# Projecting a context in 64-row tiles: three chunks of 64 dims in place of 128 and 64, and copies shared by two engines

## The chip, the cores and the metric

The kernel runs on one core of one Trainium2 chip. The metric is the time of one execution in device microseconds (us). The engines named below are TensorE (PE in the profile, with its weight loads as PEld), VectorE (DVE), ScalarE (ACT), GpSimd (POOL) and SyncE (SP, which only issues transfers here).

## The reference, cut to what matters

The program is a model of four layers over x, 128 tokens of 256 numbers. Each layer has an attention over a long context, an attention among the tokens, and experts. All is fp32.

```python
x = x + _L0_xattn_ref(_layernorm(x), ctx_768, mask, Wq, Wk, Wv, Wo)
x = x + _L0_attn_ref(...) ; x = x + _L0_ffn_ref(...)
x = x + _L1_xattn_ref(_layernorm(x), ctx_768, Wq, bq, Wk, bk, Wv, bv, Wo, bo)
...                                   # layers 1, 2 and 3 likewise
```

The context `ctx_768` has 12544 rows of 192 numbers and is the same in all layers. An attention over it makes, for 16 heads of 16 numbers (layers 0 to 2), keys = ctx @ Wk (+ bk) and values = ctx @ Wv (+ bv), both 12544 x 256, then softmax(q k) v over all 12544 rows. Layer 0 has a mask, layer 1 clips its scores, layers 1 and 2 have biases. Layer 3 has heads of 64 numbers and its own code.

## The kernel before, in words

The context is cut into 25 blocks of 512 rows (`NSB`, `SB`), the last with 256. Heads go in two groups `g` of eight, whose keys are 128 rows of numbers. For each group `attend_twice_in` goes over the blocks twice. The first pass projects keys and values of each block, keeps them in SBUF, and finds the highest score of each query. The second pass makes the exponentials and the weighted sums from the kept keys and values.

*The projection* (class `Keys`, one matmul line, L103). A block's 192 dims lie in SBUF as two tiles: `ctxA` holds dims 0 to 127 on 128 partitions, and `ctxB` holds dims 128 to 191 of the block's first 256 rows on partitions 0 to 63 and of its second 256 rows on partitions 64 to 127. `keys_into` and `values_into` are called with `low` 0 (contract over 128 partitions) and then with `low` 1 (over 64, where the matmuls of the two halves use different partitions of the array). Keys of the first 256 rows go to the left half of one PSUM bank, their values to the right half, and the second 256 rows to a second bank: the tile `pair` of two banks. `keep_keys` (L131 without bias, L133 with) and `keep_values` (L137) then copy both banks to SBUF on ScalarE. Before the first pass, `early` projects two blocks (layer 0) or eight (layers 1 and 2) ahead, through the one-pair tile `kv`, in the midst of the work of the stage before; there the context comes by POOL's queue.

*The first pass.* `steps` says which blocks each step projects: two blocks ahead, and in group 0 of layers 1 and 2 fewer than one a step, since eight are done. The last three blocks project keys alone in their step and values later (`project_values`). Products with the queries (L559, L558 with the mask) are four matmuls of 32 rows side by side. In layer 0 each block's products go to VectorE, which takes maxima (L565, four a step). In layers 1 and 2 two blocks go together: POOL subtracts their keys (`apart`, L570), PE makes products with the difference, ScalarE takes a Relu of each of two pairs (`over`, L578), PE makes products with the second block's keys, and VectorE adds and takes the maximum (L586, four a step).

*What sets the order.* Tiles and their waits come from a tile framework; within a step, `in_order` holds PE, VectorE and ScalarE to the order in which the code names the work. The PSUM tiles of the first pass are a pool of four pairs (`ppr=4`), given out in turn: in layers 1 and 2 a step takes one for the projection, two for the difference, and two for the second keys. Outside the passes a scheduler places the instructions of each engine, from its own costs.

*Transfers.* `context` loads blocks one ahead into four buffers for each of `ctxA` and `ctxB` (L395 and L397). In layer 1, `add_up` adds each block of group 0 to `sums` on POOL (L99, L100), for a test on NaN in `nan_guard`. Layer 3 (`KeysInTurn`) takes its context from the same function, two blocks ahead. SP's queue also issues layer 0's mask rows (L547, four a block) and, at the start, layer 3's small weights (`down`, L1158), which VectorE scales between its first maxima. In layer 0's experts POOL makes eight widened copies (`wide`, L1691) that PE then turns, and the expert weights come by SP's queue into ten buffers.

Of the kernel before, what the change touches and what calls it, by code (L numbers as in the profile page):

```python
# [12 lines left out]
F32 = mybir.dt.float32  # L13
# [4 lines left out]
ALU = mybir.AluOpType  # L18
# [3 lines left out]
P = 128  # L22
D = 256
CD = 192
CB = CD - P
H = 16
# [27 lines left out]
class Keys:  # L54
# [4 lines left out]
    def __init__(self, net, wk, wv, groups, bias=None, sums=None):  # L59
        self.net, self.nc, self.wk, self.wv, self.bias, self.sums = net, net.nc, wk, wv, bias, sums  # L60
        self.context = net.context(groups * NSB)
        self.started, self.done, self.rest = {}, 0, None
        if sums is not None:
            self.nc.gpsimd.memset(sums, 0.0)
# [30 lines left out]
    def add_up(self, g, b):  # L95
        if g == 0 and self.sums is not None:
            a, c = self.context(b)
            n = HB * len(self.halves(b))
            self.nc.gpsimd.tensor_tensor(self.sums[:, :n], self.sums[:, :n], a[:, :n], ALU.add)  # L99
            self.nc.gpsimd.tensor_tensor(self.sums[:, SB:], self.sums[:, SB:], c, ALU.add)  # L100
# [16 lines left out]
    def values_into(self, p, g, low, blocks, first=0, turn=None):  # L117
        cols = slice(g * P, g * P + P)
        for j, b in enumerate(blocks):
            ctx = self.context((g if turn is None else turn) * NSB + b)[low]  # L120
            for c in range(2):
                for i, r in self.halves(b):
                    at = first + (2 * j + c) * P
                    r = r if low else slice(0, P)
                    k = c * P if low else i * HB + c * P
                    self.mm(p[:, i, at : at + P], ctx[r, k : k + P], self.wv[r, low, cols], low, first + j + c == 0)

    def keep_keys(self, g, b, p):
        to = self.kT(b).rearrange("p (i k) -> p i k", i=2)[:, : p.shape[1]]
        if self.bias is None:  # L130
            self.nc.scalar.copy(to, p)  # L131
        else:
            self.nc.scalar.activation(to, p, AF.Identity, bias=self.bias[:, g : g + 1])  # L133

    def keep_values(self, g, b, p):
        to = self.v(b).rearrange("p (i c) h e -> p i (c h) e", i=2)[:, : p.shape[1], :, :16]
        self.nc.scalar.copy(to, p.rearrange("p i (h e) -> p i h e", e=16))  # L137

    def steps(self, g):

        todo = [b for b in range(2, NSB) if g * NSB + b >= self.done]
        n, at, out = len(todo), 0, []
        for t in range(NSB):
            to = min(n, -(-n * (t + 1) // (NSB - 2)))
            while to < n and todo[to] <= t + 2:
                to += 1
            out.append([(b, low, b < NSB - 3) for b in todo[at:to] for low in range(2)])
            at = to  # L150
        return out

    def project(self, g, b, low, values=True):


        if g * NSB + b < self.done:
            return
        if not low:
            self.add_up(g, b)
            self.started[g, b] = self.net.early_pair() if self.rest is None else self.net.pair()  # L160
        p = self.started[g, b]
        self.keys_into(p, g, low, [b])
        if values:
            self.values_into(p, g, low, [b], HB)
        if low:
            n = len(self.halves(b))
            self.keep_keys(g, b, p[:, :n, :HB])
            if values:
                self.keep_values(g, b, p[:, :n, HB:])
            self.done = g * NSB + b + 1  # L170

    def project_values(self, g, blocks):
        p = self.net.pair()
        for low in range(2):
            self.values_into(p, g, low, blocks)
        for j, b in enumerate(blocks):
            self.keep_values(g, b, p[:, : len(self.halves(b)), j * HB : (j + 1) * HB])


class KeysInTurn(Keys):  # L180

    def __init__(self, net, wk, wv):
        self.net, self.nc, self.wk, self.wv = net, net.nc, wk, wv
        self.context = net.context((GROUPS3 + 1) * NSB, 2)
        self.first = {}
# [17 lines left out]
class Net:  # L207
# [123 lines left out]

    def load_column(self, src, pool, name):

        t = pool.tile([P, 2], F32, tag=name, name=name, bufs=1)
        self.nc.sync.dma_start(t, src.rearrange("o (g p) -> p (o g)", p=P))
        return t
# [46 lines left out]
    def context(self, until, ahead=1):  # L383

        nc, d = self.nc, self.d
        made = []

        def get(k):  # L390
            while len(made) <= k + ahead and len(made) < until:
                b = len(made) % NSB
                n = min(SB, S2 - b * SB)
                a = self.ahead.tile([P, SB], F32, tag="ctxA", name="ctxA", bufs=4)
                self.queue.dma_start(a[:, :n], d["ctxA"][:, b * SB : b * SB + n])  # L395
                c = self.ahead.tile([P, HB], F32, tag="ctxB", name="ctxB", bufs=4)
                self.queue.dma_start(c, d["ctxB"][b])  # L397
                made.append((a, c))
            return made[k]

        return get
# [617 lines left out]
    def l0_xattn(self, x):  # L1019
        nc, d = self.nc, self.d  # L1020
        with self.tc.tile_pool(name="x0", bufs=2, reuse_waits="tile") as pool:
            wk = self.load_kv(d["L0_xattn_Wk"], D, "wk", self.lw, nc.scalar)
            keys = Keys(self, wk, None, 2)
            keys.context(0)
            keys.wv = self.load_kv(d["L0_xattn_Wv"], D, "wv", self.lw, nc.scalar)
# [14 lines left out]
    def keys_biased(self, name, guarded):  # L1040

        nc, d = self.nc, self.d
        wk = self.load_kv(d[f"{name}_Wk"], D, "wk", self.lw)
        wv = self.load_kv(d[f"{name}_Wv"], D, "wv", self.lw)
        bk = self.load_column(d[f"{name}_bk"], self.lw, "bk")
        sums = self.lw.tile([P, SB + HB], F32, tag="sums", name="sums", bufs=1) if guarded else None
        keys = Keys(self, wk, wv, 2, bk, sums)

        self.queue = nc.gpsimd
        keys.early()  # L1050
        return keys
# [33 lines left out]
    def nan_guard(self, pool, totals, xT, wq, bq, wk, wv, bk, bv):  # L1085
# [4 lines left out]
        wide = pool.tile([P, 2, P], F32, tag="wide", name="wide")  # L1090
# [5 lines left out]
        def sums():  # L1096
            s = self.stat(2)
            nc.vector.tensor_reduce(s[:, 0:1], totals[:, :SB], AX.X, ALU.add)
            nc.vector.tensor_reduce(s[:, 1:2], totals[:, SB:], AX.X, ALU.add)
            nc.vector.tensor_copy(wide, bc(s, 2, P))  # L1100
            nc.gpsimd.memset(many, float(S2))

        def products(bank_pair):
            p = bank_pair()
            self.mm(p[:, 0, :D], [(xT[:, k, :], wq[:, k, :]) for k in range(2)] + [(self.ones[:1, :], bq)])
            self.mm(p[:, 1, :D], [(wide[:, k, :], wk[:, k, :]) for k in range(2)] + [(many, bk)])
            made.append(p)
            p = bank_pair()
            self.mm(p[:, 0, :D], [(wide[:, k, :], wv[:, k, :]) for k in range(2)])
# [749 lines left out]
def layout(inputs):  # L1859
# [4 lines left out]
    ctx[:, :S2] = a["ctx_768"][0].T  # L1864
    given["ctxA"] = ctx[:P, :S2]
# [31 lines left out]
def program(given):  # L1897
    nc = bacc.Bacc("TRN2", target_bir_lowering=False, num_devices=1)
# [12 lines left out]
```

## Time and profile before

| | us |
|---|---|
| median of 3 runs | 3020.04 (3013.86 to 3021.88) |
| profiled execution: time | 3021.48 |
| profiled execution: span | 3019.8 |
| PE busy (weight loads beside it) | 2882.8 (2209.0) |
| VectorE / ScalarE / POOL busy | 2024.2 / 1626.2 / 282.7 |
| start of a regular step to the next, first pass, layer 0 | 5.62 |
| the same, layers 1 and 2 | 5.42 |
| the same, keys-only steps of layers 1 and 2 | 3.99 |

The first passes of layer 0 run from about 40 to 160 and 275 to 420, of layer 1 from 658 to 785 and 906 to 1045, of layer 2 from 1311 to 1440 and 1554 to 1697. Experts of layer 0 end at about 650, layer 3 begins at about 1930.

How to read it: a row of the timeline gives the start, the length from the first start to the last end, engine, line, operation, the tiles (out<-in), for matmuls the rows and columns of the array in use (64\*128 is 64 rows), and a count. Idle time of the engine just before it and what ended that wait stand in brackets. An fp32 matmul is two instructions, and each has its own weight load (PEld). Matmuls are pipelined: the next starts before the last has ended, so starts tell the pace.

### The profile page before, as it was taken

The numbers are of one execution on the slowest core, as the hardware profiler recorded it, in microseconds if no ns is written. First come the engines' busy times: TensorE is split into PE (matmuls) and PEld (weight loads), VectorE is DVE, ScalarE is ACT, GpSimd is POOL, SyncE is SP. The second block draws the span as 40 slices with busy tenths as digits, with TensorE's granted clock in tenths as the row PEclk, the third lists the DMA queues.
The fourth block names the chain that finished last, engine by engine and source line by source line (L and its number), as shares of the span: only waits on it lengthen the run. The fifth ranks groups of instructions, "written<-read, shape, count | busy, mean of one in ns | idle before, by whom it ended". The sixth has DMA issues, their size and how long they took to land.

```text
span 3019.8 us, 79794 instructions
## 1 busy us (share of the span) xinstructions
PE 2882.8 (95%) x34893; PEld 2209.0 (73%) x34893; DVE 2024.2 (67%) x3241; ACT 1626.2 (54%) x1904; POOL 282.7 (9%) x504
## 2 busy tenths in 40 slices
PE   8999999989999999999999998899999999999969
PEld 5677667455676576765776675688989989889858
DVE  6876887525893598745544555577777777777844
ACT  1176148335685585245875682355655656555521
POOL 7011021223001100211001002000000000000000
PEclk9999999999999999999999998999999999999979
DMA  5201210562002202521012007232322223222436
GB/s 133 61 19 32 72 39 6 189 225 57 21 3 79 59 4 88 175 82 53 15 39 73 23 3 258 92 98 80 85 84 83 85 79 88 85 78 83 136 111 201
DMA packets 177706, 247.28 MB, mean 82 GB/s; under 512 B 32459, under 2 KB 119269, under 8 KB 177358
## 3 DMA queue, kind: packets, MB, share of 16 engines
q1 hardware_dynamic: 165592, 227.26, 24.8%
q0 software_dynamic: 11008, 14.37, 1.6%
q8 instruction: 274, 4.49, 0.6%
q10 hardware_dynamic: 758, 0.55, 0.1%
q14 instruction: 74, 0.61, 0.1%
HBM read 241.56 MB, written 0.13 MB: 80 GB/s over the span
## 4 chain that ended last, share of the span: by engine, by line
PE 83%; DVE 11%; ACT 2%; DMA 1%; issue 1%; SPq 1%; POOL 0%; ACTq 0%; DVEq 0%; POOLq 0%
PE pair L103 21%; PE acc L699 10%; PE pair L559 8%; PE v L103 8%; PE sc L859 6%; PE pair L629 5%; PE acc L901 5%; PE ps L279 5%; PE one L629 4%; DVE parts L565 3%; PE pair L622 2%; PE acc L279 2%; PE kv L103 2%; PE ps L1698 1%; DVE over L586 1%
## 5 line engine op out<-in xcount | busy, mean ns | idle before, releaser
L586 DVE CUSTOM_DVE_ANT_0 over<-over,pair 128x512 f32<-128x512 f32 x384 | 241.2, 683 | 249.2 <-PE pair L559 237.6
L103 PE MATMUL pair<-ctxA,wk 128*128 128x256 f32 x1236 | 328.7, 399 | 6.5 <-ACT over L578 1.8
L103 PEld LDWEIGHTS pair<-ctxA,wk 128*128 128x128 f32 x1236 | 217.0, 190 | 138.5 <-ACT over L578 53.0
L861 ACT COPY kept<-sc 128x1024 f32<-128x1024 f32 (+1 forms) x135 | 136.2, 1009 | 261.2 <-PE sc L859 261.2
L565 DVE TENSOR_REDUCE parts<-pair 128x2 f32<-128x1024 f32 (+1 forms) x216 | 235.7, 1157 | 41.8 <-PE pair L559 41.8
L290 DVE TENSOR_TENSOR top<-top,kept 128x1024 f32<-128x1024 f32 (+2 forms) x145 | 169.1, 1169 | 134.0 <-ACT kept L861 132.7
L293 DVE SCALAR_TENSOR_TENSOR e<-pair,floor 128x1024 f32<-128x1024 f32 x196 | 227.3, 1217 | 14.6 <-PE pair L629 14.6
L677 ACT ACTIVATE e<-pair 128x1024 f32<-128x1024 f32 x196 | 200.7, 1025 | 46.5 <-PE pair L629 26.0
L654 ACT ACTIVATE e<-e 128x1024 f32<-128x1024 f32 x196 | 206.7, 1057 | 35.3 <-DVE e L293 24.3
L629 PE MATMUL pair<-qz,kT 32*128 32x256 f32 x2112 | 218.9, 374 | 0.0
L699 PE MATMUL acc<-e,v 128*17 128x128 f32 x6336 | 211.4, 274 | 3.0 <-ACT e L692 2.2
L699 PEld LDWEIGHTS acc<-e,v 128*17 128x17 f32 x6336 | 155.8, 97 | 67.8 <-ACT e L692 45.6
L692 ACT ACTIVATE e<-e 128x1024 f32<-128x1024 f32 x196 | 205.0, 1048 | 0.0
L293 DVE SCALAR_TENSOR_TENSOR e<-one,maskcol,less 128x256 f32<-128x256 f32 x392 | 162.6, 477 | 53.3 <-PE one L629 43.3
L859 PE MATMUL sc<-qz,kT 64*128 64x128 f32 x2816 | 197.8, 279 | 0.0
L559 PE MATMUL pair<-kT,qz 32*128 32x512 f32 (+1 forms) x1120 | 192.7, 592 | 5.2 <-DVE parts L586 3.8
L578 ACT ACTIVATE over<-pair 128x1024 f32<-128x1024 f32 x192 | 186.9, 1021 | 14.7 <-PE pair L559 7.4
L103 PEld LDWEIGHTS v<-wv,ctxA 128*128 128x128 f32 x1568 | 189.8, 192 | 6.4 <-issue 1.7
L103 PE MATMUL v<-wv,ctxA 128*128 128x128 f32 x1568 | 193.1, 276 | 0.0
L103 PE MATMUL pair<-ctxB,wk 64*128 64x256 f32 x1236 | 188.9, 399 | 0.0
L290 DVE TENSOR_TENSOR e<-one,less 128x512 f32<-128x512 f32 x196 | 126.3, 686 | 88.6 <-PE pair L629 88.1
L859 PEld LDWEIGHTS sc<-qz,kT 64*128 64x128 f32 x2816 | 171.6, 187 | 13.0 <-issue 1.3
(457 smaller groups left out, 5637.7 us busy)
## 6 DMA issues: line engine op xcount, KB each, us to landing
ctxA<-in_ctxA SPq DMA_DIRECT2D x324, 256.0 KB
ctxB<-in_ctxB SPq DMA_DIRECT2D x339, 128.0 KB
w<-in_L_ffn_W SPq DMA_DIRECT2D x32, 1024.0 KB
ctxA<-in_ctxA POOLq DMA_DIRECT2D x36, 256.0 KB, 3.2
w<-in_L_ffn_w_gateT SPq DMA_DIRECT2D x8, 1024.0 KB
wu<-in_L_ffn_w_upT SPq DMA_DIRECT2D x8, 1024.0 KB
w<-in_L_ffn_w_downT SPq DMA_DIRECT2D x8, 1024.0 KB
w<-in_L_ffn_w1T SPq DMA_DIRECT2D x8, 1024.0 KB
```

Of the source, the lines that this page charges most:

```text
L103: self.nc.tensor.matmul(out, a, b, start=start and not low, stop=low == 1, skip_group_check=True)
L279: self.nc.tensor.matmul(out, lhsT, rhs, start=(i == 0), stop=(i == n - 1))
L290: self.nc.vector.tensor_tensor(out, a, b, op)
L293: self.nc.vector.scalar_tensor_tensor(out, a, s, b, op0, op1, **kw)
L559: nc.tensor.matmul(x, qz[r, g, s, :], k[r, :n], start=not by_mask, stop=True)
L565: nc.vector.tensor_reduce(parts[:, s, 2 * half : 2 * half + 2, i], x, AX.X, ALU.max)
L586: nc.vector.tensor_tensor_reduce(es[half][:, j, :], es[half][:, j, :], x[:, j, :], 1.0, -LARGEST, ALU.add, ALU.max, parts[:, s, 2 * half + ...
L629: nc.tensor.matmul(at, keys.kT(c // 4)[tiles[t], k], q, start=start, stop=True, skip_group_check=True)
L654: nc.scalar.activation(to, to, AF.Exp)
L692: nc.scalar.activation(to, to, AF.Exp)
L699: nc.tensor.matmul(acc[32 * t : 32 * t + 17, half, :], v[:, c % 4 + j, 4 * half + t, :], es[half][:, t // 2, j, t % 2, :], start=c + j + h ...
L859: nc.tensor.matmul(x[:, t, c : c + P], kT[r, c : c + P], qz[r, g, :], start=True, stop=True)
```

## The change

The change splits the context's 192 dims into three chunks of 64 (`CH`) for layers 0 to 2. The host lays out a block so that partitions 0 to 63 hold the three chunks of its first 256 rows and partitions 64 to 127 those of its second 256 rows; one transfer of 128 x 768 loads it. Wk and Wv are loaded twice, once for each half of the partitions (`load_twice`). Every matmul of the projection then contracts over 64 partitions. Keys of a block are projected first (part 0), its values after them (part 1). In layers 1 and 2, within the passes, ScalarE copies the first bank (keys and values) and VectorE the second; in layer 0 and in `early` ScalarE copies both, as before. Layer 3 keeps its 128 and 64 rows (the old functions move into `KeysInTurn`), but its two context tiles become one tile of 128 x 768 with two transfers. `nan_guard` sums over three chunks. The area for descriptors of POOL's transfers is set to 8192 bytes a partition instead of the default 16384.

```diff
 CB = CD - P
+CH = CD // CB
...
     def add_up(self, g, b):
         if g == 0 and self.sums is not None:
-            a, c = self.context(b)
-            n = HB * len(self.halves(b))
-            self.nc.gpsimd.tensor_tensor(self.sums[:, :n], self.sums[:, :n], a[:, :n], ALU.add)
-            self.nc.gpsimd.tensor_tensor(self.sums[:, SB:], self.sums[:, SB:], c, ALU.add)
+            self.nc.gpsimd.tensor_tensor(self.sums, self.sums, self.context(b), ALU.add)
...
+    def keys_into(self, p, g, b):
         cols = slice(g * P, g * P + P)
+        ctx = self.context(g * NSB + b)
+        for c in range(CH):
             for i, r in self.halves(b):
+                self.mm(p[:, i, :HB], self.wk[r, c, cols], ctx[r, c, :], c == 0, c == CH - 1)
+
+    def values_into(self, p, g, b, first=0):
         cols = slice(g * P, g * P + P)
+        ctx = self.context(g * NSB + b)
+        for half in range(2):
+            at = first + half * P
+            for c in range(CH):
                 for i, r in self.halves(b):
+                    self.mm(p[:, i, at : at + P], ctx[r, c, half * P : half * P + P], self.wv[r, c, cols], at + c == 0, c == CH - 1)
+
+    def keep(self, g, b, p):
+        if self.bias is None or self.rest is None:
+            self.keep_keys(g, b, p, slice(0, len(self.halves(b))))
+            self.keep_values(g, b, p, slice(0, len(self.halves(b))))
+            return
+        for i, _ in self.halves(b):
+            self.keep_keys(g, b, p, slice(i, i + 1), on_vector=i == 1)
+            self.keep_values(g, b, p, slice(i, i + 1), on_vector=i == 1)
+
+    def keep_keys(self, g, b, p, halves, on_vector=False):
+        to, p = self.kT(b).rearrange("p (i k) -> p i k", i=2)[:, halves], p[:, halves, :HB]
+        if on_vector:
+            self.nc.vector.tensor_scalar(to, p, self.bias[:, g : g + 1], None, ALU.add)
+        elif self.bias is None:
             self.nc.scalar.copy(to, p)
         else:
             self.nc.scalar.activation(to, p, AF.Identity, bias=self.bias[:, g : g + 1])
...
+    def keep_values(self, g, b, p, halves, first=HB, on_vector=False):
+        to = self.v(b).rearrange("p (i c) h e -> p i (c h) e", i=2)[:, halves, :, :16]
+        p = p[:, halves, first : first + HB].rearrange("p i (h e) -> p i h e", e=16)
+        if on_vector:
+            self.nc.vector.tensor_copy(to, p)
+        else:
+            self.nc.scalar.copy(to, p)
...
-    def project(self, g, b, low, values=True):
+    def project(self, g, b, part, values=True):
...
-        if not low:
+        if part == 0:
             self.add_up(g, b)
-            self.started[g, b] = self.net.early_pair() if self.rest is None else self.net.pair()
+            p = self.started[g, b] = self.net.early_pair() if self.rest is None else self.net.pair()
+            self.keys_into(p, g, b)
+            return
         p = self.started[g, b]
-        self.keys_into(p, g, low, [b])
         if values:
-            self.values_into(p, g, low, [b], HB)
...
+            self.values_into(p, g, b, HB)
+            self.keep(g, b, p)
+        else:
+            self.keep_keys(g, b, p, slice(0, len(self.halves(b))))
+        self.done = g * NSB + b + 1
...
+    def load_twice(self, src, n, name, pool, queue=None):
+        v = pool.tile([P, CH, n], F32, tag=name, name=name, bufs=1)
+        for i in range(2):
+            (queue or self.nc.sync).dma_start(v[i * CB : (i + 1) * CB], src.rearrange("(c p) n -> p c n", p=CB))
+        return v
...
+                t = self.ahead.tile([P, SB + HB], F32, tag="ctx", name="ctx", bufs=4)
+                if whole:
+                    self.queue.dma_start(t, d["ctx"][b])
+                    made.append(t.rearrange("p (c k) -> p c k", c=CH))
+                    continue
                 n = min(SB, S2 - b * SB)
-                a = self.ahead.tile([P, SB], F32, tag="ctxA", name="ctxA", bufs=4)
-                self.queue.dma_start(a[:, :n], d["ctxA"][:, b * SB : b * SB + n])
-                c = self.ahead.tile([P, HB], F32, tag="ctxB", name="ctxB", bufs=4)
-                self.queue.dma_start(c, d["ctxB"][b])
-                made.append((a, c))
+                self.queue.dma_start(t[:, :n], d["ctxA"][:, b * SB : b * SB + n])
+                self.queue.dma_start(t[:, SB:], d["ctxB"][b])
+                made.append((t[:, :SB], t[:, SB:]))
...
-            self.mm(p[:, 1, :D], [(wide[:, k, :], wk[:, k, :]) for k in range(2)] + [(many, bk)])
+            self.mm(p[:, 1, :D], [(wide[:, k, :], wk[:, k, :]) for k in range(CH)] + [(many, bk)])
...
+    given["ctx"] = ctx.reshape(CH, CB, NSB, 2, HB).transpose(2, 3, 1, 0, 4).reshape(NSB, P, CH * HB)
...
-    nc = bacc.Bacc("TRN2", target_bir_lowering=False, num_devices=1)
+    nc = bacc.Bacc("TRN2", target_bir_lowering=False, num_devices=1, dynamic_dma_scratch_size=8192)
```

## The prediction, made before the changed kernel ran

> **What bounds the kernel now.** I read the page first: engine totals and the chain that ended last.
>
> ```profile
> PE 2882.8 (95%) x34893; PEld 2209.0 (73%) x34893; DVE 2024.2 (67%) x3241; ACT 1626.2 (54%) x1904; POOL 282.7 (9%) x504
> ...
> PE pair L103 21%; PE acc L699 10%; PE pair L559 8%; PE v L103 8%; PE sc L859 6%; PE pair L629 5%; PE acc L901 5%; PE ps L279 5%; PE one L629 4%; DVE parts L565 3%; PE pair L622 2%; PE acc L279 2%; PE kv L103 2%; PE ps L1698 1%; DVE over L586 1%
> ```
>
> PE carries the end, and the projection (L103 into pair) is the largest item of the chain. In order of time that chain repeats: a projection starts every 5.42 us in layers 1 and 2 and every 5.62 us in layer 0. So I read one step of layer 1 on PE (start, length, work).
>
> ```profile
> 921.19 1.13 PE L103 MATMUL pair<-ctxA,wk 128*128 128x256 f32 x4
> 922.16 1.05 PE L103 MATMUL pair<-wv,ctxA 128*128 128x128 f32 x8
> 923.14 0.70 PE L103 MATMUL pair<-ctxB,wk 64*128 64x256 f32 x4
> 923.68 0.61 PE L103 MATMUL pair<-wv,ctxB 64*128 64x128 f32 x8
> 924.22 1.14 PE L559 MATMUL pair<-apart,qz 32*128 32x512 f32 x8
> 925.18 1.50 PE L559 MATMUL pair<-kv,qz 32*128 32x512 f32 x8
> ```
>
> The projection takes 3.03 us (921.19 to 924.22). An fp32 matmul is two instructions, and 64-row matmuls run in twos. Inside a run, 128-column steps follow at 0.11 us: the full-height ones (1.05 less one 0.275)/7, the half-height twos (0.61 less 0.272)/3. A 256-column step takes 0.216. Each change of row height costs extra: the last full-height step starts at 922.94, the next row at 923.14 (0.20 instead of 0.11), and the first two of half height hold PE 0.32 instead of 0.216. Together 0.20 us a change.
>
> The copies and what waits for them, ScalarE first, then the weight loads:
>
> ```profile
> 924.34 0.69 ACT L133 ACTIVATE kv<-pair,bk 128x512 f32<-128x512 f32 x1 [2.36 <-PE pair L103]
> 924.92 0.58 ACT L137 COPY kv<-pair 128x512 f32<-128x512 f32 x1
> 925.44 1.94 ACT L578 ACTIVATE over<-pair 128x1024 f32<-128x1024 f32 x2
> ```
> ```profile
> 925.55 0.30 PEld L559 LDWEIGHTS pair<-kv,qz 32*128 32x128 f32 x4 [0.18 <-ACT kv L137]
> 926.61 0.51 PEld L103 LDWEIGHTS pair<-ctxA,wk 128*128 128x128 f32 x3 [0.76 <-ACT over L578]
> ```
>
> A step takes five two-bank tiles from four (projection, two for the differences, two for the second keys), so the last product takes the projection's own tile. It waits until both copies end (925.50) and starts at 925.55, against 925.18 for the other half. PE's second pass then starts at 926.09, and the next projection at 926.61. That next projection takes the tile that the first Relu reads (925.44 to 926.46). Had PE been early it would still have waited until 926.51. A keys-only step, which is shorter, shows that wait deciding:
>
> ```profile
> 1021.67 1.94 ACT L578 ACTIVATE over<-pair 128x1024 f32<-128x1024 f32 x2 [0.42 <-PE pair L559]
> ```
> ```profile
> 1022.74 1.13 PE L103 MATMUL pair<-ctxA,wk 128*128 128x256 f32 x4 [0.30 <-ACT over L578]
> ```
>
> The first of the two Relus ends at 1022.69, PE goes on 0.05 later. From the end of a projection to the next one this way is 2.30 us: 1.22 until the Relu starts, 1.02, 0.05.
>
> In layer 0 a step ends differently: the next projection takes the tile that the first maximum reads.
>
> ```profile
> 103.93 2.36 DVE L565 TENSOR_REDUCE parts<-pair 128x2 f32<-128x1024 f32 x2 [1.00 <-PE pair L559]
> ```
> ```profile
> 105.21 0.51 PEld L103 LDWEIGHTS pair<-ctxA,wk 128*128 128x128 f32 x3 [0.92 <-DVE parts L565]
> ```
>
> VectorE idles 1.00 us before that maximum, so a shorter projection moves it, and the next step with it.
>
> **The change part by part.**
>
> *Projection in 64-row tiles.* Twelve matmuls a block become 18 (24 instructions and weight loads become 36), but they run in twos: 6 steps of 256 columns and 12 of 128, 6 x 0.216 + 12 x 0.1115 = 2.63 us, exactly what 4 + 2 and 8 + 4 steps take now. Gone is the change from 128 to 64 rows: 2.83 instead of 3.03. Entering 64 rows straight from 32 is not in the trace; bounds are no cost and the 0.20 of 128 to 64; entering 128 from 32 costs about as much as the latter now, so I take that. That long 64-row runs hold their pace shows in layer 3:
>
> ```profile
> 2015.72 1.16 PE L859 MATMUL sc<-qz,kT 64*128 64x128 f32 x16
> 2016.71 1.03 PE L103 MATMUL pair<-ctxB,wk 64*128 64x256 f32 x8
> 2017.58 1.06 PE L103 MATMUL v<-wv,ctxB 64*128 64x128 f32 x16
> 2018.47 0.73 PE L859 MATMUL sc<-qz,kT 64*128 64x128 f32 x10
> ```
>
> The run at 2017.58, between others of its height, makes eight twos in 0.89 (0.111 each), the one at 2016.71 four of 256 in 0.87. The first, entered from 128 rows, needs 0.99.
>
> A rule that speaks against the change: the Trainium skill's "TensorE: Matmul & The Clock Gate", section "LDWEIGHTS (loading the stationary operand)", says that a load takes time by its columns, not its rows, about columns/1.2 ns. By an estimate from that page, with nothing hidden, 12 more loads of 107 ns would add 1.28 us a block, and over some 118 blocks 150 us. The rows above show twos at 0.111 us with both loads inside, and by them the block gets 0.20 shorter.
>
> *A bank each.* Now ScalarE needs 924.34 to 925.50 for both copies. Then it copies 128x256 twice: 0.47 (that form of L133) and 0.37 (of L137), about 0.75 overlapped as now. VectorE does the other bank: 0.42 each by its 128x256 copy out of PSUM (L285, 424 ns), about 0.77. Count from the projection's start: results 2.90, copies done by 3.75, +0.05 = 3.80; PE wants that tile at 2.83 + 0.96 = 3.79. The stall of 0.37 goes. VectorE's copies stand in its order before the four L586 of the step and behind those of the last step, which end 2.27 us into the step (now 923.46, 2.27 too); so they wait for PE, not the reverse. Behind them the L586, which need products that come later (about 4.9). VectorE's busy time rises from 2.7 to 3.6 of a step.
>
> *What is late next.* PE alone would repeat after 4.74 (2.83 + 0.96 + 0.95). But the Relu holds the next projection until 2.83 + 2.30 = 5.13. So a step goes from 5.42 to 5.13, not to 4.74: 0.29. Before a step without a projection, only the shorter projection counts (0.20), as that step hangs on the Relus too. Keys-only: 3.99 to 3.79.
>
> *Layer 0.* Both copies stay on ScalarE. 5.62 to 5.42; the four maxima take 4.6 and do not bind. Keys-only steps already run at 4.60 and 4.52, VectorE's own pace: nothing.
>
> *Transfers.* One load of 384 KB instead of 256 and 128: one issue of 0.33 us on SP (0.54 on POOL) fewer a block, on queues with time to spare. The buffer returns later (after the last matmul, about 1 us in a step, 3.3 us in layer 3's), but loads go to a block four on: 12 us or more to spare against 3.2 to land. The smaller descriptor area holds half as much; POOL has at most four loads open. Bounds 0 and 1 us; I take 0.
>
> *Guard.* wk and wv get a third chunk: four more PE instructions, at 4.44 us for 16 now: +1.1. One sum instead of two on POOL and VectorE: free.
>
> *Start and early projections.* The order of the built programs shows mask rows and layer-3 loads changing places on SP at the start (the chain there waits for a `down` load that lands at 38.17); in layer 0's experts POOL makes the eight `wide` copies two loads earlier, and 64-row matmuls stand alone between 128-row ones, each such island a change more. Bounds -4 and +9 (some 30 islands of 0.20, 2 MB more among the expert weights); I take 0, as both signs are there.
>
> *Sum.* Layer 0: 36 regular steps x 0.20 = 7.2. Layers 1 and 2, each: 29 x 0.29 + 4 x 0.20 + 6 keys-only x 0.20 = 10.4, so 20.8. The two blocks of group 1 that PE projects alone (6.06 us on the chain): 3 x 2 x 0.20 = 1.2. Values-only blocks: 12, half of them on the chain, 1.2. Less 1.1. In all 29.3. The profiled execution took 3021.48 (span 3019.8), 1.4 above the median: 2992.
>
> **Rivals.**
> 1. *The Relu does not hold PE.* For: on full steps PE is now later than it by 0.1. Against: the keys-only rows. 0.38 x 58 more: 2970.
> 2. *Early stages give back.* For: PE's queue is in order, and the islands. Against: there the experts wait for weights (DMA 0.90 busy from 600 to 650), the attention for VectorE. The whole +9: 3001.
> 3. *Nothing.* If entering 64 from 32 rows cost 0.20 more than entering 128, and the Relu came later by as much: within 9 us of before. Nothing in the trace speaks for it.
> 4. *Slower.* The twos are paced by their weight loads. At the 0.188 us of one load instead of 0.111 a block costs 12 x 0.077 = 0.92 more; over some 118 blocks +109: about 3100. It decides from 0.132 us a two on (29.3/118/12 = 0.021 above 0.111). Against it: layer 3's runs.
>
> **How the numbers follow.** Forecast 0.68, rival 1 0.07, rival 2 0.14, rival 3 0.05, rival 4 0.06. A measurement tells 0.3% (9 us) from no change. Faster 0.68 + 0.07 + 0.14 = 0.89, same 0.05, slower 0.06. Range: from 2977 (start at its good end, and half of rival 1) to 3007 (rival 2, the 1 us of descriptors, and the 0.09 x 58 that the bank split gives on top of the 0.20 gone).
>
> **What would show it.** Projection rows of 2.83 us, all 64*128; steps of 5.13 in layers 1 and 2 with PE waiting for the Relu some 0.3 us, of 5.42 in layer 0; the wait for the copy gone; VectorE some 0.85 us a step more. Wrong if the twos run slower than 0.12 us, if PE waits for VectorE's copy, or if the stretch from 520 to 660 grows.

## The result, and the profile after

The changed kernel takes 3049.54 us (median of 4 runs, 3043.51 to 3050.22) where the kernel before takes 3017.36 beside it. The ratio is 1.0101, with a 95% interval of 1.0081 to 1.0122. The forecast was 2992, 29 us faster; it became about 30 us slower. The profiled execution took 3043.51 (span 3041.8), 22.0 us more than that of before.

The page of the changed kernel, busy times and the chain that ended last:

```profile
PE 2898.9 (95%) x36661; PEld 2205.1 (72%) x36661; DVE 2082.8 (68%) x3384; ACT 1597.7 (53%) x1904; POOL 270.1 (9%) x461
...
PE v L201 9%; PE pair L201 8%; PE pair L101 7%; PE acc L745 6%; PE pair L605 6%; PE sc L905 6%; PE acc L947 6%; PE pair L675 4%; PE ps L314 3%; PE pair L668 2%; PE acc L314 2%; PE one L675 2%; DVE over L632 1%; PE ps L1743 1%; PE kv L101 1%
```

These totals say little: PE is at 95% as before. The stretches say where the 22 us are. A first pass is taken here from its first product to the first score of the pass after it.

| us | before | after | difference |
|---|---|---|---|
| start to the last regular step of layer 0's first pass | 138.9 | 141.1 | +2.2 |
| from there to layer 1's first product | 523.5 | 521.3 | -2.2 |
| the four first passes of layers 1 and 2 | 517.8 | 539.8 | +22.0 |
| all the rest | 1839.6 | 1839.6 | 0 |

Layer 0 did what was forecast. Its regular steps went from 5.62 to 5.42 us, but the first of them starts at 48.9 in place of 43.4, which eats the gain. All of the loss is in the first passes of layers 1 and 2, which were to gain 20.8. One step of layer 1, in order of time (start, length, work; idle time before and what ended it in brackets):

```profile
937.88 1.57 PE L101 MATMUL pair<-ctx,wk 64*128 64x256 f32 x12
939.28 1.50 PE L101 MATMUL pair<-wv,ctx 64*128 64x128 f32 x24
940.72 1.14 PE L605 MATMUL pair<-apart,qz 32*128 32x512 f32 x8
940.83 0.47 ACT L140 ACTIVATE kv<-pair,bk 128x256 f32<-128x256 f32 x1 [2.69 <-PE pair L101]
941.21 0.37 ACT L148 COPY kv<-pair 128x256 f32<-128x256 f32 x1
941.60 0.48 DVE L136 TENSOR_SCALAR kv<-pair,bk 128x256 f32<-128x256 f32 x1 [2.07 <-ACT kv L148]
942.00 0.41 DVE L146 COPY kv<-pair 128x256 f32<-128x256 f32 x1
942.53 0.33 PEld L605 LDWEIGHTS pair<-kv,qz 32*128 32x128 f32 x4 [0.66 <-issue]
943.62 0.19 PEld L101 LDWEIGHTS pair<-ctx,wk 64*128 64x128 f32 x2 [0.76 <-ACT over L624]
```

The projection is as forecast: 937.88 to 940.72, 2.84 us, one run of 64 rows. The copies are not. ScalarE copies its bank from 940.83 to 941.58, and VectorE, idle for 2.07 us, starts only at 941.60, released by ScalarE's values copy (L148). The tile is free at 942.42, 1.70 us after the projection gave way to the products; before, with both banks on ScalarE, it was 1.28 (924.22 to 925.50). The last product, which takes that tile, is loaded at 942.53, 0.11 us after it is free (the profile names no releaser for this wait of 0.66 us), and the next projection starts at 943.62. The step takes 5.74 us, not 5.13, and more than the 5.42 of before.

What VectorE waits for shows in its groups, layer 1's second group (last columns: idle time before, releaser):

```profile
L136 DVE TENSOR_SCALAR kT<-pair,bk 128x256 f32<-128x256 f32 x14 | 6.8, 484 | 29.0 <-ACT v L148 29.0
L136 DVE TENSOR_SCALAR kv<-pair,bk 128x256 f32<-128x256 f32 x8 | 3.9, 484 | 18.6 <-ACT kv L148 18.6
```

In 14 blocks keys and values are kept in separate SBUF tiles (`kT`, `v`). There VectorE's keys copy, which writes `kT`, still waits for ScalarE's values copy, which writes `v`. The one thing that both touch is the PSUM tile `pair`, and of that they read different banks. So the theory to test: the tile framework orders two engines on one PSUM tile, whatever parts of it they read; the chip doesn't ask for it. The rivals: the 64-row order of the matmuls causes it, or two engines reading PSUM together are slow in themselves.

### The profile page after: what moved, and what is told of

It reads as the page before. It is cut to its first block, busy times and chain, and to the rows that moved or that the text cites. A ratio compares the mean times of both kernels' runs of the same rounds, so it can differ in the third digit from the quotient of the medians.

```text
span 3041.8 us, 82965 instructions
## 1 busy us (share of the span) xinstructions
PE 2898.9 (95%) x36661; PEld 2205.1 (72%) x36661; DVE 2082.8 (68%) x3384; ACT 1597.7 (53%) x1904; POOL 270.1 (9%) x461
## 4 chain that ended last, share of the span: by engine, by line
PE 65%; DVE 6%; ACT 2%; issue 1%; POOL 1%; DMA 0%; POOLq 0%; ACTq 0%; SPq 0%; DVEq 0%
PE v L201 9%; PE pair L201 8%; PE pair L101 7%; PE acc L745 6%; PE pair L605 6%; PE sc L905 6%; PE acc L947 6%; PE pair L675 4%; PE ps L314 3%; PE pair L668 2%; PE acc L314 2%; PE one L675 2%; DVE over L632 1%; PE ps L1743 1%; PE kv L101 1%
## 5 line engine op out<-in xcount | busy, mean ns | idle before, releaser
L201 PEld LDWEIGHTS v<-wv,ctx 64*128 64x128 f32 (+1 forms) x3136 | 295.9, 190 | 12.2 <-issue 1.9
L201 PE MATMUL v<-wv,ctx 64*128 64x128 f32 (+1 forms) x3136 | 301.2, 275 | 0.0
L201 PE MATMUL pair<-ctx,wk 64*128 64x256 f32 (+1 forms) x1440 | 276.0, 384 | 1.4 <-ACT kT L229 1.4
L101 PEld LDWEIGHTS pair<-ctx,wk 64*128 64x128 f32 x1548 | 144.5, 190 | 120.3 <-ACT over L624 52.2
L101 PE MATMUL pair<-ctx,wk 64*128 64x256 f32 x1548 | 210.8, 400 | 10.5 <-DVE parts L611 5.2
L201 PEld LDWEIGHTS pair<-ctx,wk 64*128 64x128 f32 (+1 forms) x1440 | 192.3, 188 | 34.4 <-issue 13.2
L605 PE MATMUL pair<-kT,qz 32*128 32x512 f32 (+1 forms) x1120 | 209.8, 593 | 5.3 <-DVE parts L632 3.8
L101 PEld LDWEIGHTS pair<-wv,ctx 64*128 64x128 f32 x3096 | 201.5, 192 | 12.2 <-DVE parts L611 3.8
L101 PE MATMUL pair<-wv,ctx 64*128 64x128 f32 x3096 | 203.7, 277 | 0.0
```

Source lines behind the costliest of these rows:

```text
L101: self.nc.tensor.matmul(out, a, b, start=first, stop=last, skip_group_check=True)
L201: self.nc.tensor.matmul(out, a, b, start=start and not low, stop=low == 1, skip_group_check=True)
L605: nc.tensor.matmul(x, qz[r, g, s, :], k[r, :n], start=not by_mask, stop=True)
```

## The experiments

**The copies back on ScalarE, 64-row tiles kept** (e1).

```diff
     def keep(self, g, b, p):
-        if self.bias is None or self.rest is None:
-            ...
-            return
-        for i, _ in self.halves(b):
-            self.keep_keys(g, b, p, slice(i, i + 1), on_vector=i == 1)
-            self.keep_values(g, b, p, slice(i, i + 1), on_vector=i == 1)
+        self.keep_keys(g, b, p, slice(0, len(self.halves(b))))
+        self.keep_values(g, b, p, slice(0, len(self.halves(b))))
```

> The changed kernel with the copies as before: ScalarE copies both banks everywhere, the 64-row tiles stay. Theory: the loss lies in VectorE's copies, which start only when ScalarE's have ended. Then a full step of layers 1 and 2 is 2.83 (projection) + 1.28 (end of the projection to the end of both copies, as before) + 0.05 + 1.06 (last product's load to the next projection) = 5.22 us in place of 5.74; layer 0 stays at 5.42. Some 53 such steps: 53 x 0.52 = 28 us off the changed kernel, 3049.5 to about 3022, ratio to before about 1.001 (0.998 to 1.004). Rival: the 64-row tiles are at fault, by another wait in the step. Then the step stays above 5.4 and the time within 9 us of the changed kernel's, ratio 1.008 or more.

Measured: 3021.54 us, ratio to before 1.0006 (0.9989 to 1.0023). Its step:

```profile
940.68 1.57 PE L101 MATMUL pair<-ctx,wk 64*128 64x256 f32 x12
943.63 0.69 ACT L135 ACTIVATE kv<-pair,bk 128x512 f32<-128x512 f32 x1 [2.18 <-PE pair L101]
944.22 0.58 ACT L143 COPY kv<-pair 128x512 f32<-128x512 f32 x1
944.85 0.30 PEld L600 LDWEIGHTS pair<-kv,qz 32*128 32x128 f32 x4 [0.18 <-ACT kv L143]
945.90 0.30 PEld L101 LDWEIGHTS pair<-ctx,wk 64*128 64x128 f32 x4 [0.76 <-ACT over L619]
```

The step takes 5.22 us (940.68 to 945.90), as worked out. The 64-row tiles are not what lengthens it; they shorten it by the 0.20 that was forecast.

**The split alone, on the kernel before** (e2). `keep_keys` and `keep_values` of the 128 and 64 row kernel become, in layers 1 and 2 within the passes:

```diff
+        for i in range(n):
+            at = slice(i, i + 1)
+            ...
+            if i:
+                self.nc.vector.tensor_scalar(keys[:, at], from_keys, self.bias[:, g : g + 1], None, ALU.add)
+                self.nc.vector.tensor_copy(values[:, at, :, :16], from_values)
+            else:
+                self.nc.scalar.activation(keys[:, at], from_keys, AF.Identity, bias=self.bias[:, g : g + 1])
+                self.nc.scalar.copy(values[:, at, :, :16], from_values)
```

> The kernel before, its projection in 128 and 64 rows, with the split of the copies alone (ScalarE a bank, VectorE a bank, layers 1 and 2, in the passes). Theory: VectorE starts after ScalarE has ended, copies end 1.63 us after the projection in place of 1.28 and more hangs behind them, so the full step is the changed kernel's 5.74 plus the 0.20 of the change of row height: 5.94 us. 53 x 0.52 = 28 us more than before, ratio about 1.009 (1.006 to 1.011). Rival: the order of the two engines comes from the 64-row part (keys whole before values), and with the old order they copy side by side: step 5.33, about 5 us less than before, ratio 0.998.

Measured: 3052.89 us, ratio 1.0096 (1.0075 to 1.0116). Its step:

```profile
935.24 1.13 PE L103 MATMUL pair<-ctxA,wk 128*128 128x256 f32 x4
938.75 0.36 ACT L151 COPY kv<-pair 128x256 f32<-128x256 f32 x1
939.15 0.48 DVE L147 TENSOR_SCALAR kv<-pair,bk 128x256 f32<-128x256 f32 x1 [2.27 <-ACT kv L151]
941.17 0.30 PEld L103 LDWEIGHTS pair<-ctxA,wk 128*128 128x128 f32 x2 [0.76 <-ACT over L595]
```

The step takes 5.94 us (935.24 to 941.17) in place of 5.42. The split is the loss by itself, with the same wait, and has nothing to do with the order of the matmuls.

**The copies truly side by side** (e3). The program says that VectorE's copies have no order to ScalarE's of the same tile. They read another bank and write other places, and whoever takes the tile next still waits for all four.

```diff
+        copies = []
         for i, _ in self.halves(b):
-            self.keep_keys(g, b, p, slice(i, i + 1), on_vector=i == 1)
-            self.keep_values(g, b, p, slice(i, i + 1), on_vector=i == 1)
+            copies.append(self.keep_keys(g, b, p, slice(i, i + 1), on_vector=i == 1))
+            copies.append(self.keep_values(g, b, p, slice(i, i + 1), on_vector=i == 1))
+        for mine in copies[2:]:
+            for other in copies[:2]:
+                self.net.tc.declare_no_dep(mine.ins, other.ins, reason="reads of two banks")
```

> The changed kernel with one addition: the program declares that VectorE's two copies need not come after ScalarE's two of the same tile (they read another bank and write other places), so that no wait between the two engines is built. Theory: the wait is made by the framework for two engines on one PSUM tile, nothing on the chip needs it. Then VectorE's copy starts within 0.1 us of ScalarE's, both are done 0.9 us after the projection's end, and the full step is the predicted 5.13 us, bounded by the Relu: 53 x 0.61 = 32 us off, 3049.5 to about 3017, ratio to before 1.000 (0.997 to 1.003). Rival A: the two engines disturb each other at PSUM: copies start together but take over 0.1 us longer each (0.47 and 0.48 now), step 5.3 or more, ratio 1.003 or more. Rival B: the Relu does not hold PE either: step below 5.0, ratio below 0.997.

Measured: 3018.46 us, ratio 0.999 (0.9976 to 1.0004). Its step:

```profile
945.98 1.57 PE L101 MATMUL pair<-ctx,wk 64*128 64x256 f32 x12
948.81 1.14 PE L608 MATMUL pair<-apart,qz 32*128 32x512 f32 x8
948.93 0.47 ACT L144 ACTIVATE kv<-pair,bk 128x256 f32<-128x256 f32 x1 [2.09 <-PE pair L101]
948.93 0.48 DVE L140 TENSOR_SCALAR kv<-pair,bk 128x256 f32<-128x256 f32 x1 [0.59 <-PE pair L101]
949.30 0.36 ACT L151 COPY kv<-pair 128x256 f32<-128x256 f32 x1
949.33 0.41 DVE L150 COPY kv<-pair 128x256 f32<-128x256 f32 x1
951.11 0.30 PEld L101 LDWEIGHTS pair<-ctx,wk 64*128 64x128 f32 x4 [0.92 <-ACT over L627]
```

Both engines start at 948.93, both are done by 949.74, 0.93 us after the projection's end, and each copy takes within 0.01 us what it took alone (0.47 and 0.48, 0.36 and 0.41). The step is 5.13 us (945.98 to 951.11), the forecast to the digit, and the next projection waits for the Relu, as forecast. So the wait came from the program, and the two engines don't disturb each other. The Trainium skill, "PSUM — Partial Sum Buffer", section "PSUM bank collisions raise a hardware error", says, in our words, that two engines must be kept apart where they touch the same bank in the same group of 32 partitions, and that different banks are free. This run agrees for different banks (no run here lets two engines into the same one at once); the framework's order, which held back reads of two banks of one tile, is stricter.

Of these steps the changed kernel has 56 in its four first passes, counted by the projections' starts (the prediction took 58, the expectations 53). 56 x (5.74 - 5.13) = 34 us.

**POOL's order in layer 1** (e4). Even so e1 and e3 only draw level with before. One part of what is missing shows in the long steps of layer 1's first group (those followed by a step without a projection): 9.16 to 9.48 us in the changed kernel, 8.50 in layer 2. In e1 and e3, whose other steps are shorter, they even take 9.76 to 10.17, where before takes 8.80. The changed kernel there:

```profile
711.51 1.81 POOL L98 TENSOR_TENSOR sums<-sums,ctx 128x768 f32<-128x768 f32 x1 [4.06 <-DVE parts L632]
713.29 1.26 POOL L616 TENSOR_TENSOR apart<-kT 128x512 f32<-128x512 f32 x1
713.94 0.33 SPq L438 DMA_DIRECT2D ctx<-in_ctx  x1
714.60 1.14 PE L605 MATMUL pair<-apart,qz 32*128 32x512 f32 x8 [0.73 <-POOL apart L616]
716.96 1.82 POOL L98 TENSOR_TENSOR sums<-sums,ctx 128x768 f32<-128x768 f32 x1 [2.42 <-DMA ctx<-in_ctx]
```

POOL's sum stands ahead of the difference `apart`, and the sum waits for a load: the one issued at 713.94, after the last matmul of a projection has freed its buffer, lands for the sum at 716.96. (For the first sum the profile names VectorE, which happened to end an instruction then; of the idle time before these 15 sums it puts 51.8 us, 14 times, to the load.) Before, two buffers of 256 and 128 KB stood in its place; the larger was free 0.9 us earlier in a step (issued 2.1 us after a projection's start, now 3.0), its sum ran by itself, and the difference came 1.34 us into the projection, now 2.33.

```diff
     def add_up(self, g, b):
         if g == 0 and self.sums is not None:
-            self.nc.gpsimd.tensor_tensor(self.sums, self.sums, self.context(b), ALU.add)
+            added = self.nc.gpsimd.tensor_tensor(self.sums, self.sums, self.context(b), ALU.add)
+            if self.rest is not None and self.net.last_apart is not None:
+                info = mybir.DependencyInfo(mybir.DependencyClass.NoSync, mybir.DependencyReason.DATA)
+                self.net.tc.add_manual_dep(added.ins, self.net.last_apart.ins.name, info, reason="in order")
```

> The changed kernel with one more order on POOL: in layer 1's first pass a block's sum comes behind the last difference of two blocks' keys instead of ahead of it. Theory: in layer 1, group 0, the sum waits for a whole block's transfer (384 KB, whose buffer comes free only after the last matmul) and the difference behind it comes 0.7 us too late for PE, four or five times; that is why the long steps there take 9.2 to 9.5 us and 8.50 in layer 2, which has no sum. With the sum behind, they take 8.5 and PE waits for the difference no more: 4 to 5 us off the changed kernel, ratio to before about 1.0085. Rival: the copies are what makes these steps long; then they stay above 9.1 and the time does not move.

Measured: 3042.72 us, ratio 1.0061 (1.0044 to 1.0078). The long steps take 8.50 to 8.61 us, and PE no longer waits for the difference:

```profile
710.34 1.27 POOL L620 TENSOR_TENSOR apart<-kT 128x512 f32<-128x512 f32 x1 [6.09 <-PE pair L609]
711.57 1.83 POOL L98 TENSOR_TENSOR sums<-sums,ctx 128x768 f32<-128x768 f32 x1
714.80 1.14 PE L609 MATMUL pair<-apart,qz 32*128 32x512 f32 x8
```

The mechanism is shown. The ratio moved by 12 us where the long steps give about 3; its interval against that of the changed kernel reaches from 1 to 24 us, so the difference in size is not to be read. At the end of the pass this execution loses about 1 us again: VectorE's reduction, which the next edit moves, still stands ahead of the maxima, PE waits 3.26 us for them, and from the projection at 740.4 to the last one (786.2) it takes 45.8 us where the changed kernel takes 44.6.

**The reduction behind the last maxima** (e6, with e4's order). At the end of the same pass VectorE reduces the sum for the test on NaN. The changed kernel:

```profile
748.87 0.95 DVE L1144 TENSOR_REDUCE st<-sums 128x3 f32<-128x768 f32 x1 [3.43 <-POOL sums L98]
```
```profile
751.68 1.13 PE L605 MATMUL pair<-apart,qz 32*128 32x512 f32 x4 [1.07 <-DVE parts L632]
```

VectorE stands 3.43 us for the last sum, its maxima come late, and PE waits 1.07 us for them. Then TensorE's clock falls. The windows of 1 us (PE, PEld, VectorE, ScalarE and POOL busy, then the granted clock):

```profile
752.00:753.00 1.00, 0.91 (x6) 0.11 (x2) 1.00 (x5) 0.91 (x2) 0.05 (x1) 1.00 0.02 6
753.00:754.00 1.00, 1.00 (x6) 0.51 (x8) 0.57 (x2) 0.88 (x1) 1.00 (x1) 0.94 0.00 0
754.00:755.00 1.00, 1.00 (x6) 0.11 (x2) 0.92 (x3) 0.00 (x0) 0.22 (x1) 0.50 0.00 0
...
760.00:761.00 1.00, 1.00 (x12) 0.35 (x4) 0.00 (x0) 0.36 (x1) 0.00 (x0) 0.65 0.00 0
```

It is 0.50 from about 753.9 to 760.7, and the projection in it takes twice as long (its keys 2.93 us in place of 1.57).

```diff
-                if b == NSB - 1 and guard is not None and g == 0:
-                    guard[0]()
...
                         elif s and b < NSB - 2:
                             less = apart(i + 1)
+                    if b == NSB - 1 and guard is not None and g == 0:
+                        guard[0]()
```

> The changed kernel with POOL's order of the last run on this (the sum behind the difference), and with VectorE's reduction of the sum at the end of layer 1's first pass put behind the last maxima. Theory: in the changed kernel that reduction waits 3.4 us in VectorE's queue for the last sum, the maxima behind it come late, PE stands still for 2 us and its clock falls to 0.50 for about 5 us after it. From the projection at 740.9 to the end of that pass's projections (785.5) it takes 44.6 us where before takes 38.3. Behind the last maxima the wait costs nothing, the clock stays at 1.00 there, and the stretch falls to about 39: 6 us less, and 4 us for the sum, so some 10 us off the changed kernel, ratio about 1.007. Rival: the clock falls there for another reason than the wait; then the stretch stays above 43 us and the ratio above 1.0085.

Measured: 3044.05 us, ratio 1.0062 (1.0041 to 1.0083). The stretch from 740.8 to 779.7 takes 38.9 us as expected, at full clock:

```profile
745.00:750.00 5.00, 5.00 (x52) 3.34 (x50) 2.83 (x9) 2.30 (x4) 0.00 (x0) 1.00 0.18 69
750.00:755.00 5.00, 5.00 (x40) 2.49 (x36) 3.33 (x10) 2.85 (x5) 3.05 (x2) 1.00 0.24 79
755.00:760.00 5.00, 4.61 (x28) 1.64 (x22) 3.98 (x13) 3.85 (x4) 1.76 (x2) 1.00 0.00 0
```

The ratio is no better than e4's, though. In this execution the clock fell to half a little later, from about 781 to 791, after two other waits of PE (1.07 and 0.51 us), and the last projections of the pass took 4.62 us in place of the 2.94 that a later run (e9) shows after the same two waits, without a fall. (The changed kernel, too, shows 2.94 there.) This profiled execution is the slowest of its four, 3053.11 us.

A run that was made for something else, the next one (e5), tells the wait from the half clock. It leaves the reduction where it was, and PE waits there as well:

```profile
737.93 1.13 PE L605 MATMUL pair<-apart,qz 32*128 32x512 f32 x4 [0.75 <-DVE parts L632]
```
```profile
740.00:745.00 5.00, 4.70 (x36) 2.34 (x36) 2.86 (x9) 2.07 (x4) 0.47 (x1) 1.00 0.00 0
```

The clock stays at 1.00, and the same stretch (727.48 to 768.10) takes 40.6 us. Of the 5.7 us between 44.6 and 38.9 the wait itself is thus about 1.7, and the other 4 came with a half clock that did not follow in each execution. What the order is worth is shown for the stretch, not for the whole time.

**The start** (e5). What VectorE waits for between 15 us and the regular steps, before and then after:

```profile
DVE rate L297 <- DMA av<-in_L_xattn_v_alpha: 6.4, 1, 6.4
DVE down L297 <- DMA down<-in_L_xattn_v_downT: 3.7, 1, 3.7
```
```profile
DVE down L332 <- DMA down<-in_L_xattn_k_downT: 8.3, 1, 8.3
DVE down L332 <- DMA down<-in_L_xattn_v_downT: 4.8, 1, 4.8
```

The scalings of layer 3's small weights stand in VectorE's queue among the first maxima, in both kernels (before, the first wait is for `alpha`), but with 13.1 us of waiting now in place of 10.1, and with two maxima done ahead of the last wait in place of five. The edit moves those of `down` to POOL:

```diff
-            self.ts(self.downs[at, :], self.downs[at, :], self.rate[at, i + 1 : i + 2], None, ALU.mult)
+            nc.gpsimd.tensor_scalar(self.downs[at, :], self.downs[at, :], self.rate[at, i + 1 : i + 2], None, ALU.mult)
```

> The changed kernel with the two scalings of layer 3's small weights (down) moved from VectorE to POOL. Theory: at the start VectorE waits in order for the loads of down, 8.34 and 4.77 us in the changed kernel, ahead of layer 0's first maxima, with fewer maxima done before the last of them lands than in the kernel before; this is why the first of the regular steps starts at 48.9 us in place of 43.4. With the waits gone the first regular step starts at 36 to 45 us, 4 to 13 us earlier, and the time falls by as much: ratio to before 1.006 to 1.009. Rival: the start is bounded by the mask rows on SP's queue (0.55 us each, 4 a block); then the first regular step stays within 1 us of 48.9, and the ratio at 1.010.

Measured: 3033.91 us, ratio 1.0040 (1.0023 to 1.0058). Layer 0's last regular step starts at 132.9 in place of 141.1, 8.2 us earlier: the waits were the loss. (The 8.2 hold a difference of clock, too: from 40 to 45 us it was 0.66 in the changed kernel, and 1.00 in before and in e5.) By the ratios (1.0101 to 1.0040) it gains 18 us, but the two intervals leave anything from 7 to 30 open; the trace's 8 is the number to keep.

**All together** (e7): 64-row tiles, e3's copies, and the orders of e4, e6 and e5.

> All together: 64-row tiles, the copies side by side without a wait between the engines, the sum behind the difference, the reduction behind the last maxima, and the scalings of down on POOL. Theory: full steps of 5.13 us (32 us off the changed kernel), sum and reduction 10 us, start 4 to 13 us: 3049.5 less 46 to 55, so 2995 to 3004, ratio to before 0.993 to 0.996 and faster than both kernels. Rival: the parts are not additive, because PE that stands still less or more in one place gets its half clock in another; then the ratio is 0.997 or more.

Measured: 3000.01 us, ratio 0.9915 (0.9901 to 0.9928): 26 us faster than before by the ratio, and faster than both kernels. Its step, from one projection to the next, and what it waits for:

```profile
956.30 1.16 PEld L104 LDWEIGHTS pair<-ctx,wk 64*128 64x128 f32 x12 [0.92 <-ACT over L631]
961.43 1.17 PEld L104 LDWEIGHTS pair<-ctx,wk 64*128 64x128 f32 x12 [0.92 <-ACT over L631]
```

And its busy times:

```profile
PE 2864.8 (95%) x36661; PEld 2204.8 (73%) x36661; DVE 2081.8 (69%) x3382; ACT 1598.1 (53%) x1904; POOL 272.4 (9%) x463
```

The four first passes of layers 1 and 2 take 499.7 us where before takes 517.8 and the forecast, with its 20.8 off, came to 497.0. All full steps are 5.13 us, the long ones 8.61.

**The three orders without the change** (e8), and **with all copies on ScalarE** (e9). Both use the edits above, e8 on the kernel before, e9 on e1.

> The kernel before (128 and 64 rows, all copies on ScalarE) with the same three orders: the scalings of down on POOL, the sum behind the difference, the reduction behind the last maxima. It shows what these are worth without the change. Theory: before loses at the start too, but less; the start gains 3 to 8 us, the other two next to nothing (its long steps already take 8.80 and its stretch 38.3 us): ratio to before 0.997 to 0.999. The rest up to the 0.9915 of the run with all together, 17 to 23 us, is then the change itself with its copies side by side (predicted: 20.8 + 7.2 + 1.3 = 29 us). Rival: the three orders alone make the gain; then the ratio is 0.994 or less and the change with its copies side by side is worth less than 8 us.

Measured for e8: 3021.36 us, ratio 1.0002 (0.9991 to 1.0013). The orders bring the old kernel nothing that can be measured; I had expected 3 to 8 us. Its last regular step of layer 0 starts only 2.2 us earlier (136.7), because the wait for `alpha` (6.7 us there) stays on VectorE. So the 0.87% between e8 and e7, 26 us, is the change itself with its obstacles gone.

> The 64-row tiles with all copies on ScalarE and the three orders. It shows what sharing the copies is worth once both engines copy side by side. Theory: the step is 5.22 us in place of 5.13, in some 53 steps 5 us: ratio to before 0.993 (0.9915 to 0.9945). Rival: VectorE has more to do elsewhere because of the copies and the sharing is worth nothing; then the ratio is 0.9915 or less.

Measured for e9: 3002.61 us, ratio 0.9941 (0.9926 to 0.9957), with steps of 5.22 us. Sharing the copies, once they run side by side, gives 0.0026 more, about 8 us by the ratios, where the steps give 56 x 0.09 = 5. The two intervals overlap a little, and the four passes of the profiled executions don't show it (500.0 us in e9, 499.7 in e7, where some 10 us at half clock end the first of them), so the size of this part stays open. Most of the gain, about 18 of 26 us, comes from the 64-row tiles.

## Why the prediction was wrong

- **The 64-row tiles: right.** The projection takes 2.84 us (forecast 2.83), layer 0's step 5.42 (5.42), the keys-only step 3.80 (3.79). The rule weighed against it, that a weight load takes its columns and not its rows (the Trainium skill's "TensorE: Matmul & The Clock Gate", section "LDWEIGHTS (loading the stationary operand)"), would have made a block 1.28 us longer by an estimate from that page with nothing hidden; the measurement decides against the "nothing hidden". Rivals 3 and 4 are out.
- **"A bank each": the step that failed.** The forecast had "copies done by 3.75" into the step, with ScalarE and VectorE side by side. They were done at 4.54 (937.88 to 942.42), one engine after the other, and PE's wait for VectorE's copy, which the prediction named as what would make it wrong, took the place of the stall that was to go. No row that the prediction shows has two engines on one PSUM tile, and the cost of that was taken as zero and not bounded. Its other end is one engine after the other. The prediction's "results 2.90" is 0.05 short by its own rows (924.34 less 921.19, less 0.20, is 2.95), though its 3.75 came out as 3.76 in e3. So the far end is 2.95 + 0.75 + 0.77 = 4.47, then 0.05 and the 1.06 from the last product's load to the next projection: a step of 5.58, slower than the 5.42 of before. The step was worth 34 us.
- **The Relu as the next bound: right** once the copies run side by side (5.13 measured). Rival 1 is out.
- **Transfers, taken as 0 with a bound of 1 us: mis-sized.** It was seen that the buffer returns about 1 us later in a step, but only PE's use of the block was weighed, 12 us of slack. POOL sums the block as soon as it lands, and the difference is queued behind that sum. The four long steps of layer 1 lost 0.7 to 1.0 us each (about 3 in all), and the reduction behind the last sum cost 5.7 us of its stretch (44.6 against e6's 38.9), of which 4 came with the half clock and not in each execution (e5: 40.6).
- **The start, taken as 0 with -4 to +9: +5.5,** by the change of places among VectorE's waits that the prediction had pointed to without pricing it. Of rival 2, the start came about, at 5.5 of its 9 us.
- **The sum.** Forecast 29.3 off; the profiled executions show 22.0 more, a miss of 51. Of that the copies are 34, sum and reduction 9, the start 5.5; the rest is 2 to 3, not followed further. By the medians the miss is larger, 3049.54 against 2992: the profiled execution of the changed kernel is the fastest of its four.

The chance of a slower kernel had been set at 0.06, for a mechanism that didn't happen. The range ended at 3007 without the far end of the shared copies; with it, 0.45 us on 58 steps, it would have reached some 3033, and 3049.54 lies beyond that, too, since the measured step was 5.74 and sum and start came on top.

What stays open: whether the smaller area for POOL's descriptors costs anything. It wasn't tried alone.

## What to carry to other kernels

Before two engines share one PSUM tile, ask who orders them: a tile framework may put one behind the other though they read different banks, and then the split costs the sum of both instead of the larger. Price every engine pair that the old trace doesn't show together from both sides, with "one after the other" as the far end. When a buffer returns later, look at every engine that reads it, and at what is queued behind each, not only at the engine that carries the end.

## What was not expected of the hardware

A wait of 1.07 us on PE, with PE busy for most of the time around it, was followed by 6.8 us at a clock of 0.50 (753.9 to 760.7); in e5 a wait of 0.75 us at the same place was followed by none. The same pair of waits (1.07 and about 0.5 us) at the end of layer 1's first pass was followed by a half clock in e3, e6 and e7, and by none in e9 or the changed kernel itself.

The clock records of the traces show a grid: in each run the stretches of half clock all start a multiple of 3.41 us apart, and all but the last, which the end of the record cuts off, last a multiple of 3.41 us. The Trainium skill's "TensorE: Matmul & The Clock Gate", section "What's actually happening", tells of an activity window of about 3.4 us that runs freely and doesn't start with the work. The 6.8 us are two such steps. That it depends on where a wait falls in this grid would fit both observations, though no run here tests it.

A short wait can so cost several times its length in one execution and nothing in the next. The times of one kernel go with the clock: e5's seven executions run from 3025.15 us at a mean clock of 0.978 to 3045.45 at 0.970, in the order of their clocks.
